# A graph network with a spectral convolution on Trainium2: an earlier third tap step, taps three tiles ahead, one copy moved to ScalarE, and tap spectra stored by pairs of frequencies

## The chip, the cores and the metric

The kernel runs on one core of one Trainium2 chip. The metric is device time in microseconds (us) of one execution of the whole program, everything in float32. A core has five engines with a queue of instructions each: TensorE (PE, matrix products; PEld is its loading of weights), VectorE (DVE), ScalarE (ACT), GpSimd (POOL) and SyncE (SP). SP and ScalarE also issue DMA transfers between DRAM and the on-chip memory (SBUF); the rows "SPq" and "ACTq" of a profile are such issues, and the transfers themselves run beside the engines. TensorE writes into PSUM, which has eight banks of 128 x 512 numbers. Engines run in order, each by its own queue, and wait for each other by semaphores.

## What is computed

x has 128 graphs of 128 nodes with 256 features, adj is 128 x 128 x 128. Cut to what matters here:

```python
# layer 0
h    = maximum(layernorm(x), 0)
c    = relu(bn1(conv1d(h, conv1_w)))            # 1 tap: a product over features
c    = bn2(conv1d(c, conv2_w, pad=8))           # 17 taps along the nodes, 256 -> 256
xc   = relu(c + h)
s    = h @ w_se.T + b_se;  A = exp(-dist(s)) * adj
xn   = A @ relu(h @ w_msg.T + b_msg)            # "x_nmp"
gi   = concat(xc, xn) @ w_ih.T + b_ih;  gh = h @ w_hh.T + b_hh
r, z = sigmoid(gi_r + gh_r), sigmoid(gi_z + gh_z)
x    = x + (1 - z) * tanh(gi_n + r * gh_n) + z * h
# layer 1: graph convolutions on five groups of the first 25 nodes
h    = maximum(layernorm(x), 0)
x    = x + sum_g softmax(fusion_w)[g] * graph_conv(graph_conv(h[:, g], W1[g]), W2[g])
```

## The kernel before

The graphs are handled in 32 blocks of four (`BB`). Layer 0 has three stages.

**Front.** The 17-tap convolution is done in the frequency domain, with windows of 80 points (`LW`) and so 40 pairs of real coefficients (`NP_`). For the first 64 graphs (16 blocks) each block goes through these helpers: `head_load` (x from DRAM, tile `ln`, five blocks ahead), `head_stats` (mean and variance on VectorE, L191 to L194, and a power by GpSimd, L196, tile `rs`), `head_norm` (VectorE, L202, four instructions), `head_turn` (eight transposes on TensorE, L212, and a ReLU by ScalarE, L213, into `ht`, which is also stored, L214), `head_conv1` (L226, with weights `wc1`) and `head_spectra` (L241, transform into the large tile `X`; L247 and L249 copy it from PSUM by VectorE and ScalarE).

Between these, the spectra of the taps are made, which fill TensorE while the blocks wait for other engines. There are eight tap tiles (c, q): 128 of the input channels and 64 of the output channels. `taps_load` brings a tile of taps (`w2`, 1 MB, two buffers), `weight_spectra` turns it in four steps of 16 products (L165, 32 records in the profile; only 17 of the array's 128 rows are used). Of each step's four banks three are evicted by ScalarE (L173) and one by VectorE (L171), and in the last step all four by ScalarE. After the last step ScalarE issues the store of the tile's spectra `sp` (2.5 MB) to the DRAM tensor `vd` (L175), and behind it the load of the next-but-one tile's taps (L155). `some_spectra` does one such step. `constants()` folds the batch norm into `wc1` and other constants; its first part runs on VectorE and GpSimd (L126 to L134, two powers of GpSimd, L128), its second needs TensorE (L138), ScalarE (L139) and VectorE (L140, L141). `constant_loads` issues three small loads on SP, `vec` (all biases and norms) among them.

In this stage all orders are written out by hand: the instructions stand in each engine's queue in the order of the calls.

**Spectral.** For each of 40 frequencies TensorE multiplies `X` with the tap spectra (L302, L312, L317: three complex-product terms). The spectra of two frequencies at a time come back from `vd` (L294, tile `v`, two loads of 512 KB, three buffers); GpSimd forms the sum `vs` (L309). The results go to DRAM (`yd`). Then the 64 other graphs pass through the heads and the spectral stage again. The heads of the second half begin within the first spectral stage.

**Gates.** A planner orders the rest. For each block: `messages` (L516; VectorE adds biases and forms `lr`, L517 to L529), `conv_out` (L498, L501, back from the frequency domain), `edge_terms` (L536, transposes of `lr`), `edges` (L548, and L553 on VectorE), `x_nmp` (L563; the result `xn` has two halves c, copied from PSUM by ScalarE for c = 0, L568, and by VectorE for c = 1, L566), `gate_inputs` (L586 to L589, tile `t`) and `gates` (L612, seven products of a Strassen scheme for each gate). `degrees` (L698 to L722) works out layer 1's degrees on VectorE beside the first block: long reductions of tensors that SP has just begun to load (`dga`, `dgb`, `dgc`).

Of the kernel before, what the change touches and what calls it, by code (L numbers as in the profile page):

```python
# [8 lines left out]
F32 = mybir.dt.float32  # L9
# [4 lines left out]
P = 128  # L14
# [6 lines left out]
LW = 80  # L21
# [53 lines left out]
def gnn_kernel(ctx: ExitStack, tc: tile.TileContext, io, out0: bass.AP, out1: bass.AP):  # L75
# [19 lines left out]
    def row(name, n):  # L95

        return bass.AP(tensor=io[name].tensor, offset=io[name].offset, ap=[[0, P], [1, n]])
# [14 lines left out]
    brz = cst.tile([P, 4], F32)  # L112

    def constant_loads():
        nc.sync.dma_start(vec, io["vec"])
        nc.sync.dma_start(wc1, io["wc1"].rearrange("(c p) o -> p c o", p=P))
        nc.sync.dma_start(fd, io["fd"])

# [27 lines left out]


    htd = [dram.tile([P, C, T], F32, tag=f"ht{i}", name=f"htd{i}") for i in range(NBLK)]
    vd = dram.tile([C, D // WCH, P, LW, WCH], F32, tag="vd", name="vd")
    yd = [dram.tile([HG, 2, LW, D], F32, tag=f"yd{h}", name=f"yd{h}") for h in range(NH)]  # L150

    def taps_load(pool, c, q, queue, split=1):
        w2 = pool.tile([P, WCH // 4, P], F32, tag="w2", name="w2", bufs=2)
        for t in range(0, WCH // 4, WCH // 4 // split):
            queue.dma_start(w2[:, t:t + WCH // 4 // split], io["w2t"][:, c, q, t:t + WCH // 4 // split])  # L155
        return w2

    def weight_spectra(pool, c, q, w2):

        sp = pool.tile([P, LW, WCH], F32, tag="sp", name="sp", bufs=2)  # L160
        for t in range(WCH // 16):
            ps = [bank() for _ in range(4)]
            for j in range(4):
                for r in range(4):
                    nc.tensor.matmul(ps[r][:, j * LW:(j + 1) * LW], w2[32 * r:32 * r + KW, 4 * t + j, :],  # L165
                                     gt[32 * r:32 * r + KW, :], start=True, stop=True)
            for r in range(4):
                o0 = t * 16 + 4 * r
                dst, s = sp[:, :, o0:o0 + 4], ps[r][:, :4 * LW].rearrange("p (j d) -> p d j", j=4)
                if r == 3 and t < WCH // 16 - 1:  # L170
                    nc.vector.tensor_copy(dst, s)  # L171
                else:
                    nc.scalar.copy(dst, s)  # L173
            yield
        nc.scalar.dma_start(vd[c, q], sp)  # L175


    xs, stats, hcs, h1s = {}, {}, {}, {}
# [5 lines left out]
    def head_stats(wk, i, behind=None):  # L184

        mv = wk.tile([P, BB, 2], F32, tag="mv", name="mv", bufs=3)
        st = wk.tile([P, BB, 6], F32, tag="st", name="st", bufs=2)
        if behind is not None:
            nc.scalar.copy(st[:, :, 0], behind[:, :, 0])
        for b in range(BB):  # L190
            nc.vector.bn_stats(st[:, b, :], xs[i][:, b, :])  # L191
            nc.vector.bn_aggr(mv[:, b, :], st[:, b, :])
        ve = wk.tile([P, BB], F32, tag="ve", name="ve", bufs=2)
        nc.vector.tensor_scalar(ve, mv[:, :, 1], EPS, None, op0=ALU.add)  # L194
        rs = wk.tile([P, BB], F32, tag="rs", name="rs", bufs=3)
        nc.gpsimd.tensor_tensor(rs, ve, mhalf, op=ALU.pow)  # L196
        stats[i] = mv, rs
# [87 lines left out]
    def spectral(bp, X, h, amid):  # L285

        for p0 in range(0, NP_, 4):
            amid.get(p0, lambda: None)()
            ys = bp.tile([P, 4, 2, D], F32, tag="ys", name="ys", bufs=2)
            for p in range(p0, p0 + 4):  # L290
                if p % 2 == 0:
                    v = bp.tile([P, C, D // WCH, 4, WCH], F32, tag="v", name="v", bufs=3)
                    for c in range(C):
                        nc.sync.dma_start(v[:, c], vd[c, :, :, 2 * p:2 * p + 4, :].rearrange("q i d o -> i q d o"))  # L294
                vr, vi = v[:, :, :, 2 * (p % 2), :], v[:, :, :, 2 * (p % 2) + 1, :]
                a, d = X[:, :, p, 0, :], X[:, :, p, 1, :]
                y = ys[:, p - p0]
                ps = bank()
                if p == 0:
                    for k, (u, w) in enumerate(((a, vr), (d, vi))):  # L300
                        for c in range(C):
                            nc.tensor.matmul(ps[:, k * D:(k + 1) * D], u[:, c], w[:, c], start=c == 0, stop=c == C - 1)  # L302
                    nc.scalar.copy(y.rearrange("p k o -> p (k o)"), ps)
                    continue

                s = bp.tile([P, C, P], F32, tag="s", name="s", bufs=2)
                nc.vector.scalar_tensor_tensor(s, a, -2.0, d, op0=ALU.mult, op1=ALU.subtract)  # L307
                vs = bp.tile([P, C, D // WCH, WCH], F32, tag="vs", name="vs", bufs=3)
                nc.gpsimd.tensor_tensor(vs, vr, vi, op=ALU.add)  # L309
                p1 = bank()  # L310
                for c in range(C):
                    nc.tensor.matmul(p1[:, :D], a[:, c], vs[:, c], start=c == 0, stop=c == C - 1)  # L312
                k1 = bp.tile([P, D], F32, tag="k1", name="k1", bufs=2)
                nc.scalar.copy(k1, p1[:, :D])
                for k, (u, w) in enumerate(((s, vi), (d, vr))):
                    for c in range(C):
                        nc.tensor.matmul(ps[:, k * D:(k + 1) * D], u[:, c], w[:, c], start=c == 0, stop=c == C - 1)  # L317
                nc.vector.tensor_tensor(y, ps.rearrange("p (k o) -> p k o", k=2),
                                        k1[:, None, :].to_broadcast([P, 2, D]), op=ALU.add)
            for w in range(2):  # L320
                nc.scalar.dma_start(yd[h][:, w, 2 * p0:2 * p0 + 8, :].rearrange("g d o -> g (d o)"),
                                    ys[w * HG:(w + 1) * HG].rearrange("p a k o -> p (a k o)"))
# [20 lines left out]
    with front as es:  # L343
# [7 lines left out]
        with ExitStack() as ws:  # L351

            ws.enter_context(tc.manual_schedule())

            xk = ws.enter_context(tc.tile_pool(name="xk", bufs=1, side="right"))
            wp = ws.enter_context(tc.tile_pool(name="wp", bufs=1))
            ahead = 5
            todo = [(c, q) for c in range(C) for q in range(D // WCH)]
            nc.scalar.dma_start(gt, io["gt"])
            taps = [taps_load(wp, *todo[0], nc.sync, split=4)]  # L360
            head_load(xk, ahead, 0, nc.scalar)
            spectra = []

            def some_spectra(k=1):
                for _ in range(k):
                    if not spectra and todo:
                        spectra.append(weight_spectra(wp, *todo.pop(0), taps.pop(0)))
                    if spectra and next(spectra[0], STOP) is STOP:
                        spectra.pop(0)
                        if len(todo) > 1:  # L370
                            taps.append(taps_load(wp, *todo[1], nc.scalar))
                        some_spectra()

            constant_loads()
            head_load(xk, ahead, 1, nc.sync)
            taps.append(taps_load(wp, *todo[1], nc.sync))
            for k in range(2, ahead):
                head_load(xk, ahead, k, nc.sync)
            nc.sync.dma_start(fw, row("fw", 5))
            head_stats(hk, 0)  # L380
            some_spectra()
            head_norm(0)
            some_spectra()
            head_turn(hk, 0)
            consts = constants()
            next(consts)
            some_spectra()
            head_stats(hk, 1)
            some_spectra()
            next(consts)  # L390
            head_norm(1)
            head_stats(hk, 2)
            some_spectra()
            heads(hk, xk, ahead, X, 0, some_spectra)
            while spectra or todo:
                some_spectra()
# [159 lines left out]
    def x_nmp(i):  # L556

        e, msg = A_s.pop(i), msgs.pop(i)
        xn = wk.tile([P, C, T], F32, tag="xn", name="xn", bufs=2)
        for c in range(C):  # L560
            ps = bank()
            for b in range(BB):
                nc.tensor.matmul(ps[:, b * N:(b + 1) * N], msg[:, b, c * P:(c + 1) * P], e[:, b, :],  # L563
                                 start=True, stop=True)
            if c:
                nc.vector.tensor_copy(xn[:, c, :], ps)  # L566
            else:
                nc.scalar.copy(xn[:, c, :], ps)  # L568
            yield
        xns[i] = xn  # L570
# [597 lines left out]
```

## Time and profile before

| | us |
|---|---|
| median of 3 runs (1916.35 to 1928.1) | 1919.29 |
| the profiled execution | 1919.48 |
| its span | 1917.7 |

The busy time of TensorE by stage, from the view of windows (us, of the span's start):

| stage | window | TensorE busy | VectorE busy | ScalarE busy | DMA share |
|---|---|---|---|---|---|
| front, first half | 0 to 173.3 | 160.55 of 173.30 | 113.24 | 88.02 | 0.81 |
| spectral, first half | 173.3 to 279.5 | 105.23 of 106.20 | 55.34 | 16.01 | 0.84 |
| heads, second half | 279.5 to 383 | 101.73 of 103.50 | 78.02 | 47.42 | 0.54 |
| spectral, second half | 383 to 489.5 | 105.72 of 106.50 | 50.54 | 16.52 | 0.81 |
| first block of the gates | 489.5 to 550 | 56.88 of 60.50 | 46.76 | 22.15 | 0.72 |
| the rest | 550 to 1917.7 | 1360.23 of 1367.70 | 960.04 | 530.39 | 0.33 to 0.37 |

How to read it: TensorE is busy nearly all the time, so time is lost where it is idle, and where its matmuls are slow: the same matmul takes twice as long in some places. A row of a timeline gives start, duration, engine, line, operation, output and inputs, how many, and in brackets the idle time before it and what ended it. "issue" means that the profile shows nothing that was waited for.

### The profile page before, as it was taken

To read this page: it belongs to the slowest core of one execution; us is meant where nothing else is said; L and a number is where in the kernel's file an instruction comes from. 1 tells how busy PE (TensorE), PEld (TensorE's weight loads), DVE (VectorE), ACT (ScalarE), POOL (GpSimd) and SP (SyncE) were. 2 spreads that over 40 slices of the span, in tenths; PEclk is the share of its full clock that TensorE was granted. 3 is DMA by queue.
4 is the path that set the end of the run, shared out by engine and by line. 5 is a ranking of instruction groups with operands and counts; after the bars stand their busy time and mean duration, and the time that the engine had idled before them with its cause. 6 is when DMAs were issued, how large, how long until landed. Compare 5 with 4: busy or idle time off the path is not lost.

```text
span 1917.7 us, 30432 instructions
## 1 busy us (share of the span) xinstructions
PE 1890.3 (99%) x10610; PEld 1646.4 (86%) x10610; DVE 1303.9 (68%) x3247; ACT 720.5 (38%) x1555; POOL 609.1 (32%) x678
## 2 busy tenths in 40 slices
PE   8999999999999999999999999999999999999998
PEld 7888889988788888888888888888888888888887
DVE  5676557744677777777666677777756677787643
ACT  4553114411333343343343443333343434334334
POOL 1012531255234334433322233433322233443300
PEclk9999999999999999999999999999999999999999
DMA  8786896379842333333234433233334434222135
GB/s 322 288 312 226 297 311 235 121 241 306 256 117 73 74 95 76 81 90 106 71 94 97 130 97 87 73 82 108 75 90 97 144 72 107 65 78 71 36 92 151
DMA packets 248872, 265.81 MB, mean 139 GB/s; under 512 B 106866, under 2 KB 223943, under 8 KB 244239
## 3 DMA queue, kind: packets, MB, share of 16 engines
q1 hardware_dynamic: 236639, 196.70, 36.9%
q10 hardware_dynamic: 12080, 67.16, 9.0%
q8 instruction: 85, 1.39, 0.3%
q14 instruction: 68, 0.56, 0.1%
HBM read 178.66 MB, written 85.14 MB: 138 GB/s over the span
## 4 chain that ended last, share of the span: by engine, by line
PE 88%; DMA 4%; DVE 4%; issue 2%; ACT 1%; POOL 1%; SPq 0%; ACTq 0%; POOLq 0%; DVEq 0%
PE bank L612 45%; PE bank L317 6%; PE bank L516 5%; PE bank L937 5%; PE bank L877 5%; PE bank L226 4%; PE bank L312 3%; PE bank L563 3%; PE bank L498 3%; PE bank L241 3%; PE bank L165 2%; PE bank L501 1%; PE bank L788 1%; PE bank L856 1%; DMA v<-vd 1%
## 5 line engine op out<-in xcount | busy, mean ns | idle before, releaser
L612 PE MATMUL bank<-t,sw 128*128 128x256 f32 x1152 | 291.6, 380 | 0.7 <-DVE u L504 0.7
L625 POOL TENSOR_TENSOR u<-u,m 128x256 f32<-128x256 f32 x128 | 93.2, 728 | 612.7 <-ACT m L623 545.0
L612 PEld LDWEIGHTS bank<-t,sw 128*128 128x128 f32 x1152 | 215.8, 191 | 31.1 <-issue 2.3
L612 PE MATMUL bank<-t,wih 128*128 128x256 f32 x768 | 197.2, 379 | 0.0
L612 PEld LDWEIGHTS bank<-t,wih 128*128 128x128 f32 x768 | 143.4, 190 | 19.3 <-issue 0.5
L309 POOL TENSOR_TENSOR vs<-v 128x512 f32<-128x512 f32 x78 | 101.3, 1318 | 114.8 <-DMA v<-vd 49.4
L516 PE MATMUL bank<-wms,ht 128*128 128x259 f32 x512 | 124.1, 385 | 0.0
L226 PE MATMUL bank<-wc,ht 128*128 128x256 f32 x512 | 121.4, 391 | 1.6 <-ACT ht L213 1.6
L612 PE MATMUL bank<-xn,wih 128*128 128x256 f32 x384 | 114.9, 381 | 3.6 <-DVE xn L566 3.6
L612 PE MATMUL bank<-t,whh 128*128 128x256 f32 x384 | 115.0, 381 | 0.0
L612 PE MATMUL bank<-xc,wih 128*128 128x256 f32 x384 | 114.8, 381 | 0.0
L937 PE MATMUL bank<-w,hh 128*125 128x256 f32 (+9 forms) x480 | 113.5, 380 | 1.0 <-DVE hh L882 1.0
L226 PEld LDWEIGHTS bank<-wc,ht 128*128 128x128 f32 x512 | 98.0, 196 | 16.7 <-ACT ht L213 3.5
L516 PEld LDWEIGHTS bank<-wms,ht 128*128 128x128 f32 x512 | 98.3, 192 | 15.1
L612 PE MATMUL bank<-ht,whh 128*128 128x256 f32 x384 | 109.9, 380 | 0.0
L877 PE MATMUL bank<-ax,w 128*128 128x500 f32 (+8 forms) x416 | 107.0, 396 | 0.7 <-DMA w<-in_w_dram 0.7
L520 ACT ACTIVATE msg<-msg 128x512 f32<-128x512 f32 x64 | 40.3, 630 | 174.1 <-DVE msg L517 174.1
L630 DVE TENSOR_TENSOR u<-bank,u 128x256 f32<-128x256 f32 x128 | 53.7, 420 | 73.6 <-PE bank L612 73.5
L196 POOL TENSOR_TENSOR rs<-ve,mhalf 128x4 f32<-128x4 f32 x32 | 32.3, 1009 | 217.8 <-DVE ve L194 217.8
L307 DVE SCALAR_TENSOR_TENSOR s<-X 128x256 f32<-128x256 f32 x78 | 47.3, 612 | 79.4 <-PE bank L317 79.1
L937 PEld LDWEIGHTS bank<-w,hh 128*125 128x125 f32 (+9 forms) x480 | 84.3, 177 | 19.2 <-DVE hh L882 1.4
L657 ACT ACTIVATE nn<-nn,vec 128x512 f32<-128x512 f32 x64 | 46.2, 722 | 133.4 <-DVE nn L656 133.4
(187 smaller groups left out, 4279.5 us busy)
## 6 DMA issues: line engine op xcount, KB each, us to landing
v<-vd SPq DMA_DIRECT2D x80, 512.0 KB
vd<-sp ACTq DMA_DIRECT2D x8, 2560.0 KB
yd<-ys ACTq DMA_DIRECT2D x40, 512.0 KB
w<-in_w_dram SPq DMA_DIRECT2D x40, 512.0 KB
htd<-ht ACTq DMA_DIRECT2D x32, 512.0 KB
ht<-htd SPq DMA_DIRECT2D x32, 512.0 KB
ym<-yd SPq DMA_DIRECT2D x32, 512.0 KB
xt<-in_xT_dram SPq DMA_DIRECT2D x32, 512.0 KB
```

The costliest lines, as they stand in the source:

```text
L226: nc.tensor.matmul(pv[:, bb, :], ht[:, c, b * N:(b + 1) * N], wc1[:, c, :], start=c == 0, stop=c == C - 1)
L241: nc.tensor.matmul(ps[:, bb * 2 * LW:(bb + 1) * 2 * LW], h1[:, 2 * h + bb, c * P:(c + 1) * P], fd, start=True, stop=True)
L309: nc.gpsimd.tensor_tensor(vs, vr, vi, op=ALU.add)
L312: nc.tensor.matmul(p1[:, :D], a[:, c], vs[:, c], start=c == 0, stop=c == C - 1)
L317: nc.tensor.matmul(ps[:, k * D:(k + 1) * D], u[:, c], w[:, c], start=c == 0, stop=c == C - 1)
L498: nc.tensor.matmul(ps[:, b * N:(b + 1) * N], ym[:, b, o * P:(o + 1) * P], idm, start=b == 0, stop=False)
L516: nc.tensor.matmul(ps[:, :D + 3], ht[:, c, b * N:(b + 1) * N], wms[:, c, :], start=c == 0, stop=c == C - 1)
L563: nc.tensor.matmul(ps[:, b * N:(b + 1) * N], msg[:, b, c * P:(c + 1) * P], e[:, b, :], start=True, stop=True)
L612: nc.tensor.matmul(ps, w, d, start=n == 0, stop=n == len(pairs) - 1)
L625: nc.gpsimd.tensor_tensor(got["u4"], got["u2"], got["m5"], op=ALU.add)
L877: nc.tensor.matmul(pv[:, q - q0, :], w1s[k5 + g][:, c, q * P:(q + 1) * P], xv[:, c], start=c == 0, stop=c == C - 1)
L937: nc.tensor.matmul(ps[:n1, :D], hh[:, q, at:at + n1], w2s[k5 + g][:, q, :], start=q == 0, stop=q == HID // P - 1)
```

## The change

Four edits, all but one in the front stage:

- The load of `vec` goes from SP to ScalarE's queue, behind `gt`. The first part of `constants()` comes ahead of the first tap step and of `head_norm(0)`; a third tap step comes ahead of the first transposes, and the step that stood after `constants()` goes.
- The tap tiles have three buffers and are loaded three ahead: one more load on SP in the beginning, and then each tile's end issues the load of the tile after the next two.
- `vd` is laid out by pairs of frequencies: a load of `v` reads 4 KB in a row for each of 128 partitions (before: four pieces of 1 KB); the store of a tile writes 20 pieces of 1 KB for each partition (before: one of 20 KB).
- For block 0, ScalarE copies both halves of `xn`.

```diff
@@ constant_loads @@
-        nc.sync.dma_start(vec, io["vec"])
@@ vd, taps_load @@
-    vd = dram.tile([C, D // WCH, P, LW, WCH], F32, tag="vd", name="vd")
+    vd = dram.tile([C, NP_ // 2, P, D // WCH, 4, WCH], F32, tag="vd", name="vd")
...
-        w2 = pool.tile([P, WCH // 4, P], F32, tag="w2", name="w2", bufs=2)
+        w2 = pool.tile([P, WCH // 4, P], F32, tag="w2", name="w2", bufs=3)
@@ weight_spectra @@
-        nc.scalar.dma_start(vd[c, q], sp)
+        nc.scalar.dma_start(vd[c, :, :, q].rearrange("u i d o -> i u (d o)"), sp.rearrange("p (u d) o -> p u (d o)", d=4))
@@ spectral @@
-                        nc.sync.dma_start(v[:, c], vd[c, :, :, 2 * p:2 * p + 4, :].rearrange("q i d o -> i q d o"))
+                        nc.sync.dma_start(v[:, c], vd[c, p // 2])
@@ front @@
             nc.scalar.dma_start(gt, io["gt"])
+            nc.scalar.dma_start(vec, io["vec"])
...
-                        if len(todo) > 1:
-                            taps.append(taps_load(wp, *todo[1], nc.scalar))
+                        if len(todo) > 2:
+                            taps.append(taps_load(wp, *todo[2], nc.scalar))
...
             nc.sync.dma_start(fw, row("fw", 5))
+            taps.append(taps_load(wp, *todo[2], nc.sync))
             head_stats(hk, 0)
+            consts = constants()
+            next(consts)
             some_spectra()
             head_norm(0)
             some_spectra()
+            some_spectra()
             head_turn(hk, 0)
-            consts = constants()
-            next(consts)
-            some_spectra()
             head_stats(hk, 1)
@@ x_nmp @@
-            if c:
+            if c and i:
                 nc.vector.tensor_copy(xn[:, c, :], ps)
```

In the built program TensorE's order differs only there (48 products of tap steps ahead of the first transposes, and 16 behind them). On VectorE L202 of block 0 now follows L126 to L134 and the first L171; around the first block of the gates the planner also moved the sums of `dgc` and `dgb`: the one of `dgb` stands ahead of the messages, three of `dgc` behind `lr`, and two scalings of `ae` ahead of L553.

## The prediction, before the changed kernel was run

> **What bounds the kernel.** I read the shares of busy time first, then TensorE's waits, then the timeline around each long wait. The profiled execution took 1919.48 us (span 1917.7 and 1.8 around it); the median of the three runs is 1919.29, so the two bases agree to 0.2 us, and every sum below starts from 1919.5.
>
> ```profile
> span 1917.7 us, 30432 instructions
> ...
> PE 1890.3 (99%) x10610; PEld 1646.4 (86%) x10610; DVE 1303.9 (68%) x3247; ACT 720.5 (38%) x1555; POOL 609.1 (32%) x678
> ```
>
> TensorE is idle for only 1917.7 - 1890.3 = 27.4 us. The change removes no matmul, so what it can win is part of these 27 us, and what a pause costs afterwards (below). TensorE's waits over the whole span, longest first (total us, times, longest):
>
> ```profile
> PE bank L165 <- DMA gt<-in_gt_dram: 3.9, 1, 3.9
> PE bank L612 <- DVE xn L566: 3.6, 1, 3.6
> PE bank L212 <- issue: 2.6, 1, 2.6
> PE bank L165 <- DMA w<-in_w2t_dram: 2.4, 1, 2.4
> PE bank L241 <- ACT X L249: 2.3, 1, 2.3
> ```
>
> The change aims at the second (xn), third (first transposes), fourth (taps) and perhaps fifth (tap spectra). The timeline of TensorE around the fourth (start, us, what, idle before it) shows that a pause costs more than itself:
>
> ```profile
> 66.42 1.09 PE L212 MATMUL bank<-ident,ln 128*128 128x128 f32 x8
> 69.94 1.13 PE L165 MATMUL bank<-gt,w 17*128 17x80 f32 x32 [2.42 <-DMA w<-in_w2t_dram]
> 71.00 4.11 PE L241 MATMUL bank<-fd,h 128*128 128x160 f32 x16
> ```
>
> The same 16 L241 matmuls took 2.44 us at 58.27: the pause of 2.42 us cost another 1.67 us of slow matmuls.
>
> **The Trainium skill.** (1) "TensorE: Matmul & The Clock Gate", Part 1, "What's actually happening": TensorE runs at half clock by default and after an idle window of about 3.4 us, at full clock after about 3.4 us of activity. The trace agrees on the factor (eight transposes: 2.25 us at 10.25, 1.09 at 66.42), but here already 2.4 us of pause brings the slow clock. (2) "DMA: Bandwidth & Descriptors", "Why small descriptors are slow (HBM only)": each packet carries a fixed overhead of about 3 cycles. The trace agrees in direction: the view of DMA traffic shows 126 packets of 20 KB (the tap spectra's store) and then 721 of mostly 1 KB (x loads) as
>
> ```profile
> DMA packets 126, 2.58 MB, mean 430 GB/s; under 512 B 0, under 2 KB 0, under 8 KB 0
> DMA packets 721, 0.74 MB, mean 368 GB/s; under 512 B 16, under 2 KB 718, under 8 KB 720
> ```
>
> (3) Same page, "Issuing engines are not separate DMA queues": all queues share 16 DMA engines. The trace agrees: from 149 to 151 us only ScalarE's queue moved data, though SP had issued three v loads from 148.57 on.
>
> **Part 1: three tap steps first, constants earlier, vec on ScalarE's queue.** Before, TensorE does two steps (3.90 to 7.62), waits for the normalised first block and turns it at 10.25. A third step is 32 records at the slow 58 ns, 1.86 us, which fits the hole of 2.6. But the order on VectorE changes too: constants() now stands before head_norm(0). VectorE before:
>
> ```profile
> 9.73 1.38 DVE L202 TENSOR_SCALAR ln<-ln,mv,rs 128x256 f32<-128x256 f32 x4 [0.83 <-POOL rs L196]
> ...
> 11.43 0.15 DVE L126 TENSOR_SCALAR bnve<-vec 128x2 f32<-128x2 f32 x1
> ...
> 14.31 0.42 DVE L134 COPY bnb<-bn 128x512 f32<-128x512 f32 x1
> ```
>
> From L126 to the end of L134 are 3.3 us, with two round trips to GpSimd (0.7 us each), and one 0.48 us copy L171. In the new order the chain starts after L194 (8.5 us), its first pow queues behind rs (8.66 to 9.69) and starts at 9.7; so bnb ends near 12.8, L171 near 13.3, and L202 starts near 13.2 instead of 9.73: +3.5 us. vec must have landed by 8.5; issued 1.2 us in, behind gt (landed 3.90, 3.2 us after its issue), it should. ln0 is issued 0.43 later on ScalarE's queue, but waits for the first taps' data anyway: up to +0.3. The transposes then start near 13.7; what follows them is one step shorter (1.86). conv1 (L226) of block 0 starts 3.5 - 1.86 = **1.6 us later**. Bounds 0 and +3. TensorE is busy for 9.75, 9.90 and 9.23 of the ten microseconds each from 10 to 40, so it stays lost. SP issues one load fewer before wc1 and one more (1 MB of taps, 0.33 to 0.43 us) behind fw at 10.5; SP's next loads wait for L212 anyway (103.8 us of such waits), so this costs nothing while x is five blocks ahead.
>
> **Part 2: taps three tiles ahead.** At 56.21 ScalarE issues 1 MB of taps just behind the 2.5 MB store of 55.84; it lands near 69.9, 13.7 us later, and TensorE waits. One tile earlier (a tile is some 17 us) the load is hidden by a whole tile of work: **-2.42 - 1.67 = -4.1 us**; bounds -4.1 and -1. Next late would be a bank, 0.2 to 0.4 us.
>
> **Part 3: spectra by two frequencies.** A v load goes from 512 pieces of 1 KB to 128 of 4 KB, the store from 128 of 20 KB to 2560 of 1 KB. Taking 430 GB/s for the large pieces and 357 (the v loads' own 0.54 MB in 1.5 us from 152) for 1 KB, a v load falls from 1.47 to 1.22 us, 80 of them by 20 us of DMA time; but TensorE idles only 106.20 - 105.23 and 106.50 - 105.72 in the two spectral stages, 1.8 us in all, some of it for VectorE. I take **-0.6** (0 to -1.8). The store goes from 6.1 to 7.1 us at 368 GB/s. That counts once: the chain of waits has
>
> ```profile
> 139.26 9.29 DMA vd<-sp
> 148.57 6.21 DMA v<-vd
> ```
>
> and then L249 at 155.25, for which TensorE waits 2.33 us: +1.0 for the store and -0.5 for the two loads, **+0.5** (-1 to +4, if 1 KB writes to DRAM are slower than the 1 KB reads measured).
>
> **Part 4: xn by ScalarE.** ScalarE is idle from 501.0 to 503.05, so the copy is free there. VectorE before:
>
> ```profile
> 507.02 1.53 DVE L698 TENSOR_REDUCE dinv<-dga 128x53 f32<-128x1325 f32 x1 [5.18 <-DMA dga<-in_adjF_dram]
> 508.47 0.68 DVE L566 COPY xn<-bank 128x512 f32<-128x512 f32 x1
> ```
>
> The copy stood behind a reduction that waits for a load. TensorE lost 3.58 us there and then 2.9 us to the slow clock: the 16 records from 509.21 to 515.53 took 6.3 us instead of 16 x 0.216 = 3.5. But this is not all won: L586 to L589 (t from xn), the messages' evictions L517 and lr still stand behind L698, and L536 needs lr. From 508.47 until lr is done (L529, 518.65) VectorE works 10.2 us with one wait of 1.19, and from 515 to 530 it is over 99% busy. Its chain shortens by the copy (0.61 us from start to start), by the 1.2 us of waiting for dgc (the longer dgb sum now fills it) and, for lr alone, by three of the sums (0.6) that move behind it; the edge product L553 has two scalings more before it (0.5). So lr comes some 2.4 us earlier and L553 some 1.3, and TensorE, which reaches L536 earlier still, waits there and cools again: **-1.5** (0 to -6.4).
>
> **Sum.** +1.6 - 4.1 - 0.6 + 0.5 - 1.5 = -4.1: 1915.4, **1915 us**. This case's own range is 1910 to 1919.
>
> **Rivals.** *Slower: the store fills ScalarE's queue.* SP's run of v loads at 148.57 took 0.4 to 0.5 us an issue for three, then 1.22 and 2.70: roughly 100 pieces per DMA engine are taken in, then the issuer is held. The new store is 2560/16 = 160; some 60 x 16 must move first, 0.98 MB, 2.7 us at 368 GB/s, plus 0.7 until data flows: 3.4 us in which ScalarE evicts nothing. One such hold is in the trace:
>
> ```profile
> 36.53 0.45 ACTq L175 DMA_DIRECT2D vd<-sp  x1
> 37.02 2.00 ACTq L155 DMA_DIRECT2D w<-in_w2t_dram  x1
> 39.12 1.08 ACT L173 COPY sp<-bank 128x320 f32<-128x320 f32 x3 [2.98 <-issue]
> ```
>
> It cost TensorE 1.25 us idle and 1.5 us slow (L226 in 5.13 instead of 3.62), 2.75. Seven more stores at that price are 19 us, half of them absorbed 10: -4 + 10 = +6, 1925, up to 1934. It decides from two held stores on (2 x 2.75 exceeds 4.1). Against it: at 55.84 and 103.99 the pair of issues took 0.8 us, and a store's issue so far costs 0.33 whatever its 2.5 MB. *All bubbles close:* part 1 at 0, parts 2 to 4 near their good ends (-4.1, -1.8, -1, -3) and the hold at 37 us gone (-2.75): -12.6, 1907. For it: ScalarE's evictions; against it: the order on VectorE. *Nothing moves:* part 2 saved, part 1 and the later store take it back: 1918 to 1920.
>
> **Chances.** Main case 0.50, held stores 0.25, all bubbles 0.13, nothing 0.12. 1% (19 us) is about what a measurement of this kernel tells from no change. Below 1900 needs 19 of the 27 idle us with their slow matmuls, 0.10; above 1938.5 needs every store held or slow writes beside, 0.12. Leaving out a tenth on each side gives 1905 to 1930.
>
> **What would show it.** Right: no wait L165 on in_w2t; L202 near 13.2 us and L212 still waiting 3 to 4 us; L536 waiting for lr; v loads of 4 KB near 430 GB/s. Wrong: ScalarE's issue rows of taps or htd at 2 us or more behind each store, with TensorE's waits on L173 or L249; a wait on xn gone without another in its place; slow matmuls in new places.

## The result, and the profile after

| | us |
|---|---|
| kernel before, median of 6 runs | 1918.63 |
| changed kernel, median of 6 runs (1934.82 to 1940.13) | 1937.24 |
| ratio after / before, with its 95% interval | 1.009 (1.0067 to 1.0113) |
| profiled execution after, its span | 1939.18, 1937.4 |

The changed kernel is 18.6 us (0.9%) slower, where 1915 was predicted and 1905 to 1930 given as the range. The page of the changed kernel begins

```profile
span 1937.4 us, 30432 instructions
...
PE 1897.4 (98%) x10610; PEld 1652.5 (85%) x10610; DVE 1308.0 (68%) x3246; ACT 720.8 (37%) x1556; POOL 610.6 (32%) x678
```

The span grew by 19.7 us: TensorE is idle for 40.0 us instead of 27.4, and busy for 7.1 us more with the same 10,610 matmuls, which therefore ran slower. TensorE's waits, longest first (us in total, times, longest one), name new things. The waits for xn and for the taps are gone; line numbers in the front stage are one lower than before.

```profile
PE bank L164 <- ACT sp L172: 9.5, 4, 3.8
PE bank L211 <- DMA ln<-in_x_dram: 6.2, 1, 6.2
PE bank L225 <- ACT ht L212: 4.8, 6, 1.9
PE bank L164 <- DMA gt<-in_gt_dram: 4.0, 1, 4.0
PE bank L537 <- DVE lr L530: 2.5, 1, 2.5
```

Four waits of 9.5 us in all are for ScalarE's copies of the tap spectra out of PSUM. ScalarE's timeline around the second store shows why (start, us, what, idle before it):

```profile
41.44 0.33 ACTq L213 DMA_DIRECT2D htd<-ht  x1
41.81 0.45 ACTq L174 DMA_DIRECT2D vd<-sp  x1
42.35 5.35 ACTq L154 DMA_DIRECT2D w<-in_w2t_dram  x1
47.75 1.08 ACT L172 COPY sp<-bank 128x320 f32<-128x320 f32 x3 [6.33 <-issue]
```

The store's own issue takes 0.45 us. The *next* issue, the taps, takes 5.35, and the copy behind it starts only then. TensorE needs that copy's bank:

```profile
44.05 0.41 PE L164 MATMUL bank<-gt,w 17*128 17x80 f32 x2 [0.36 <-DVE X L246]
48.23 1.99 PE L164 MATMUL bank<-gt,w 17*128 17x80 f32 x26 [3.76 <-ACT sp L172]
50.15 5.36 PE L225 MATMUL bank<-wc,ht 128*128 128x256 f32 x16
```

It idles for 3.76 us, and its matmuls are slow for 7 us after that: the 16 L225 take 5.36 us instead of 3.62, and the mean granted clock is 0.67 from 45 to 50 us and 0.65 from 50 to 55, where it is 1.00 from 40 to 45. The other taps issues behind a store take 3.92, 3.30, 4.86 and 3.42 us.

The start of conv1 (L226 before, L225 after), block by block, says where the 19.7 us arose:

| point | later than before, us | what lies ahead of it |
|---|---|---|
| block 0 | 4.25 | first transposes late |
| block 1, then 2 | 5.28, then 9.29 | held issue of 5.35 |
| block 3, then 4 | 9.51, then 14.04 | held issue of 3.30 |
| block 5 | 9.93 | the old pause for the taps is gone: -4.1 |
| block 6, then 7 | 13.92, then 19.87 | held issues of 4.86 and 3.42 |
| blocks 8 to 12 | 19.6 to 19.9 | stores with no taps load behind them |
| first spectral matmul | 22.0 | last store, and an htd issue of 3.40 behind it |
| first matmul of the gates | 20.4 | two spectral stages |
| end | 19.7 | gates |

The other large item is the start. VectorE's timeline after:

```profile
8.73 0.43 DVE L190 BATCH_NORM_STATS2 st<-ln 128x6 f32<-128x256 f32 x1 [8.73 <-DMA ln<-in_x_dram]
...
15.70 1.37 DVE L201 TENSOR_SCALAR ln<-ln,mv,rs 128x256 f32<-128x256 f32 x4
```

The first x block landed at 8.73 us; before it was 6.08. The stage that loads the spectra did as intended. The chain of waits around the last store gives the durations of the store and of the first v load:

```profile
158.88 10.14 DMA vd<-sp
169.04 4.82 DMA v<-vd
```

### The profile page after: what moved, and what is told of

It is laid out like the page before. It is cut to its first block, busy times and chain, and to the rows that moved or that the text cites. A ratio compares the mean times of both kernels' runs of the same rounds, so it can differ in the third digit from the quotient of the medians.

```text
span 1937.4 us, 30432 instructions
## 1 busy us (share of the span) xinstructions
PE 1897.4 (98%) x10610; PEld 1652.5 (85%) x10610; DVE 1308.0 (68%) x3246; ACT 720.8 (37%) x1556; POOL 610.6 (32%) x678
## 4 chain that ended last, share of the span: by engine, by line
PE 88%; DVE 4%; DMA 3%; issue 2%; ACTq 1%; ACT 1%; POOL 0%; SPq 0%; POOLq 0%; DVEq 0%
PE bank L613 44%; PE bank L316 7%; PE bank L517 5%; PE bank L938 5%; PE bank L878 4%; PE bank L225 4%; PE bank L311 3%; PE bank L564 3%; PE bank L499 3%; PE bank L240 2%; PE bank L164 1%; PE bank L502 1%; PE bank L789 1%; PE bank L857 1%; PE bank L211 1%
## 5 line engine op out<-in xcount | busy, mean ns | idle before, releaser
L613 PEld LDWEIGHTS bank<-t,wih 128*128 128x128 f32 x768 | 144.0, 191 | 19.6 <-issue 0.5
L225 PE MATMUL bank<-wc,ht 128*128 128x256 f32 x512 | 123.7, 396 | 4.8 <-ACT ht L212 4.8
L225 PEld LDWEIGHTS bank<-wc,ht 128*128 128x128 f32 x512 | 99.0, 198 | 21.3 <-ACT ht L212 7.6
L306 DVE SCALAR_TENSOR_TENSOR s<-X 128x256 f32<-128x256 f32 x78 | 55.6, 716 | 75.2 <-PE bank L316 75.0
L938 PEld LDWEIGHTS bank<-w,hh 128*125 128x125 f32 (+9 forms) x480 | 84.3, 178 | 19.6 <-DVE hh L883 1.9
```

What stands on the lines that cost most here:

```text
L225: nc.tensor.matmul(pv[:, bb, :], ht[:, c, b * N:(b + 1) * N], wc1[:, c, :], start=c == 0, stop=c == C - 1)
L613: nc.tensor.matmul(ps, w, d, start=n == 0, stop=n == len(pairs) - 1)
L938: nc.tensor.matmul(ps[:n1, :D], hh[:, q, at:at + n1], w2s[k5 + g][:, q, :], start=q == 0, stop=q == HID // P - 1)
```

## The experiments

Each kernel was timed in turn with the kernel before; the ratio is against it, since its median moved between 1918.1 and 1919.6 from batch to batch.

| run | median us | ratio to before | interval |
|---|---|---|---|
| a1_old_layout | 1915.34 | 0.998 | 0.9968 to 0.9992 |
| a2_layout_alone | 1934.56 | 1.0082 | 1.0053 to 1.0111 |
| c1_taps_first | 1930.7 | 1.0063 | 1.0042 to 1.0085 |
| a4_store_on_sp | 1910.74 | 0.9958 | 0.9945 to 0.997 |
| e1_old_layout_sp | 1909.28 | 0.9955 | 0.9941 to 0.9969 |
| d3_pieces_2k | 1926.15 | 1.0038 | 1.0023 to 1.0052 |
| d1_sp_vec_back | 1908.67 | 0.9949 | 0.9932 to 0.9966 |
| d2_sp_late_consts | 1903.72 | 0.9924 | 0.9906 to 0.9942 |
| e2_sp_two_steps | 1905.4 | 0.993 | 0.9916 to 0.9945 |
| t_taps_alone | 1913.85 | 0.9976 | 0.9968 to 0.9985 |
| x_xn_alone | 1918.95 | 0.9996 | 0.998 to 1.0012 |

The theory at the outset: the store of 2560 pieces holds the next issue of its queue, and on ScalarE that blocks the eviction of PSUM. The rival: writing 1-KB pieces takes the bandwidth that the loads need.

### Is it the layout? Taken out, and put in alone

The changed kernel with the old `vd`:

```diff
-    vd = dram.tile([C, NP_ // 2, P, D // WCH, 4, WCH], F32, tag="vd", name="vd")
+    vd = dram.tile([C, D // WCH, P, LW, WCH], F32, tag="vd", name="vd")
...
-        nc.scalar.dma_start(vd[c, :, :, q].rearrange("u i d o -> i u (d o)"), sp.rearrange("p (u d) o -> p u (d o)", d=4))
+        nc.scalar.dma_start(vd[c, q], sp)
...
-                        nc.sync.dma_start(v[:, c], vd[c, p // 2])
+                        nc.sync.dma_start(v[:, c], vd[c, :, :, 2 * p:2 * p + 4, :].rearrange("q i d o -> i q d o"))
```

> The changed kernel with the tap spectra in the old layout (store 128 pieces of 20 KB, loads of 1 KB pieces); start, taps and xn as changed. Held issues (theory): ScalarE's issue of the taps behind each store falls from 3.3 to 5.4 us to at most 2, the four pauses of TensorE before L164 (9.5 us, with their slow matmuls about 15 to 18) go, and the time is 1919 to 1923. Start (rival: constants and vec cost most of it): 1933 to 1936. Bandwidth (rival: the small pieces load the DMA engines): also 1919 to 1923, so this run tells the layout from the rest, not held issues from bandwidth.

Measured 1915.34. In its trace the taps issues behind the stores take 0.39 to 1.70 us, and no wait of L164 for L172 is left. The kernel before with the three opposite lines and nothing else:

> The kernel before with the new layout of the tap spectra alone. Held issues: five to six taps issues of 3 to 5 us behind the stores, TensorE waits on L173, and the taps still come late once; 1932 to 1940. Start (rival): 1917 to 1919. Bandwidth (rival): 1925 to 1940, with TensorE waiting for data (taps, ln) and not for ScalarE's copies.

Measured 1934.56. Its taps issues behind the stores take 3.33 to 5.52 us, and TensorE's longest wait is

```profile
PE bank L165 <- ACT sp L173: 10.1, 4, 3.9
```

The late taps that were also expected are not there: no wait for the taps is left in this run. Between them the two runs settle the place: the layout alone costs 0.8% (15.9 us; taken out of the changed kernel it is worth 21.9), all the rest together gains 0.2%. The first came out 4 us below its expectation. At conv1 of block 0 it is 4.7 us behind the kernel before; by block 3 it has won back 2.3 (the issue that took 2.00 us in the kernel before takes 0.60), at block 5 the taps' 4.1 more, and at the first spectral matmul it is ahead (171.48, against 173.14).

### Bandwidth or held issue? The store on another queue, and another order

```diff
-        nc.scalar.dma_start(vd[c, :, :, q].rearrange(...
+        nc.sync.dma_start(vd[c, :, :, q].rearrange(...
```

> The changed kernel with the eight stores of spectra issued by SP and no longer by ScalarE; pieces, layout and bytes as in the change. Held issues: SP is held now and computes nothing, ScalarE's taps issues are back at 0.4 to 1 us, the pauses before L164 go: 1918 to 1924. Bandwidth (rival): the same pieces run on the same 16 DMA engines, so nothing is won: 1934 to 1938. Start (rival): 1934 to 1938.

Measured 1910.74: the same bytes in the same pieces, and 26.5 us less. That is 7 us below the range expected; at the first spectral matmul this run is 28.8 us ahead of the changed kernel, so the held issues had cost more than was thought. The traffic while a store is under way is alike in both, first the changed kernel (45 to 47 us), then this one (42 to 44):

```profile
DMA packets 751, 0.77 MB, mean 386 GB/s; under 512 B 1, under 2 KB 750, under 8 KB 751
```

```profile
DMA packets 756, 0.77 MB, mean 387 GB/s; under 512 B 0, under 2 KB 756, under 8 KB 756
```

So the rival falls. The hold is not gone but has moved to SP, whose next issue, an x load, is now the long one, while ScalarE's taps issue takes 1.23 us. SP's timeline, then ScalarE's:

```profile
39.26 0.37 SPq L174 DMA_DIRECT2D vd<-sp  x1
39.73 7.11 SPq L181 DMA_DIRECT2D ln<-in_x_dram  x1
```

```profile
40.68 1.23 ACTq L154 DMA_DIRECT2D w<-in_w2t_dram  x1
```

SP computes nothing and is several x blocks ahead, so nobody waits for these 7 us.

The other order keeps both issues on ScalarE, the taps load ahead of the store:

```diff
             yield
+        if len(todo) > 2:
+            taps.append(taps_load(pool, *todo[2], nc.scalar))
         nc.scalar.dma_start(vd[c, :, :, q].rearrange(...
```

> The changed kernel with the load of the next taps issued ahead of the store of the spectra, both by ScalarE as before; nothing else. If what is held is the issue that follows the store (theory), the issue that follows is now one of htd some 6 to 17 us later, which finds the queue free: no issue over 1.5 us but the last (htd behind the eighth store, about 3.4 us), 1918 to 1924. If the store's own issue is what holds ScalarE, or bandwidth, it stays at 1933 to 1938.

Measured 1930.7, which misses both ranges, and the trace shows what the expectation overlooked. ScalarE's timeline around the third store:

```profile
58.41 0.34 ACTq L154 DMA_DIRECT2D w<-in_w2t_dram  x1
58.84 0.39 ACTq L176 DMA_DIRECT2D vd<-sp  x1
...
61.57 5.97 ACTq L215 DMA_DIRECT2D htd<-ht  x1
67.58 1.08 ACT L172 COPY sp<-bank 128x320 f32<-128x320 f32 x3 [6.05 <-issue]
```

The taps issue is short, and htd, 2.7 us behind the store, is held in its place. Behind the second store htd came 9.9 us later, at 51.99, and took 0.78. So it is whichever issue comes next on that queue while the store is being moved.

### Is it the number of pieces? 1280 of 2 KB

```diff
-    vd = dram.tile([C, NP_ // 2, P, D // WCH, 4, WCH], ...)
+    vd = dram.tile([C, NP_ // 4, P, D // WCH, 8, WCH], ...)
...
-                        nc.sync.dma_start(v[:, c], vd[c, p // 2])
+                        nc.sync.dma_start(v[:, c], vd[c, p // 4, :, :, 2 * (p % 4):2 * (p % 4) + 4])
```

(The store is cut with d=8 to match.)

> The changed kernel with the spectra in DRAM by four frequencies: ScalarE's store has 1280 pieces of 2 KB (80 per DMA engine) where it had 2560 of 1 KB (160), the same bytes; each v load is 512 pieces of 1 KB again. If a queue takes in about 100 pieces per DMA engine and holds the next issue until older ones are moved, most of the following taps issues (128 pieces, 8 more per engine) are not held: 1 us or less each, TensorE's waits on sp L172 in the front stage below 2 us together, and a time of 1912 to 1918. If it is scattered writing or pieces under some size that holds the issue, about half of each hold stays (2 us behind several stores) and the time is 1924 to 1930. If the hold went by bytes, nothing would change: 1934 to 1940.

The holds behaved as the count says: the five taps issues took 0.68, 1.63, 0.74, 1.00 and 0.77 us, 4.8 in all, where they took 20.9, and TensorE's waits on L172 fell from 9.5 to 0.9 us. The longest:

```profile
43.34 1.34 ACTq L174 DMA_DIRECT2D vd<-sp  x1
44.77 1.63 ACTq L154 DMA_DIRECT2D w<-in_w2t_dram  x1
```

The time, 1926.15, is nevertheless outside the 1912 to 1918 of this theory and inside the 1924 to 1930 of the other. The trace puts the rest elsewhere: its first x block landed at 10.79 us, and from the first spectral matmul to the gates it took 324.2 us, the changed kernel 314.8. There TensorE waited for GpSimd's sums of v (5.5 us in six waits), in the first spectral stage at

```profile
231.77 1.91 PE L311 MATMUL bank<-vs,X 128*128 128x256 f32 x4 [2.04 <-POOL vs L308]
```

The v loads, four pieces of 1 KB at steps of 2 KB, take 0.62 us each to issue (median) instead of 0.35. So the median alone would have named the wrong theory; the issue rows tell them apart. This profile is the slowest of nine executions, so how much of the 324.2 us belongs to the kernel is not known.

The pieces of this run are also twice as large, so a limit by size would do as well here. Against it speaks the run of v loads in the prediction: three loads of 1-KB pieces were taken in before the fourth was held. The changed kernel's own trace narrows the count. While its third taps issue was held (65.77 to 69.07), ScalarE's queue (q10) moved

```profile
q10 hardware_dynamic: 1014, 1.04, 88.8%
```

that is 1014 of the store's 2560 pieces. When the issue got through, 1546 were left, 97 per engine; for the fifth it was 94, close to the "roughly 100" of the prediction's rival. It is not one fixed number: on SP, the hold of 7.11 us ended with 47 per engine left.

### What the layout is worth where no one is held

The changed kernel with the old layout *and* the store on SP, `nc.sync.dma_start(vd[c, q], sp)`:

> The changed kernel with the spectra in DRAM as before (128 pieces of 20 KB for a store, 512 of 1 KB for a v load) and the store on SP's queue; against the run with the new layout and the store on SP (1910.7) it prices the layout alone, with no issue held on ScalarE. Theory: the 4-KB loads are worth 0.6 to 1.8 us in the spectral stages as predicted, and a few held issues that the old store too put on ScalarE go: 1911.5 to 1913. Rival: nearly all of what the store on SP brought against the old layout on ScalarE (1915.3 to 1910.7) is the layout's: 1914.5 to 1916. Second rival: the layout is worth nothing once the store is off ScalarE: 1910 to 1911.

Measured 1909.28, against 1910.74 with the new layout; the ratios, 0.9955 and 0.9958, can't be told apart. The time lies below all three ranges, nearest the second rival: the layout brings nothing to the median that these runs can tell. Taking the store off ScalarE does, with the old layout too: 0.998 to 0.9955. The run with the old layout on ScalarE has a wait of 2.9 us for ScalarE's copy L248 behind the last store, which is absent with either store on SP. In the profiled executions the spectral part is shorter with 4-KB loads (314.1 to 315.8 us in seven kernels, 316.3 to 323.1 in the five with the old layout), but those are one execution each, and the one of e1 was the slowest of its ten.

### The start

With the store on SP, `vec` is loaded by SP again:

```diff
     def constant_loads():
+        nc.sync.dma_start(vec, io["vec"])
...
-            nc.scalar.dma_start(vec, io["vec"])
```

> The changed kernel with the store on SP's queue and the 128-piece load of vec back at the head of SP's constants. Theory: the vec issue ahead of it delayed the first x load by 0.45 us, enough to fall behind SP's wc1, so that it lands at 6.1 us again where it landed at 8.2 to 8.7; the first normalisation L201 then starts near 13.2 us and the first transposes near 13.8, conv1 of block 0 at 21 to 21.7 us (it was 23.7 with the store on SP), and the time is 2 to 2.7 us below the kernel with the store on SP alone: 1908 to 1909. Rival: the x load is late because of the taps ahead of it, whatever vec does: it lands at 8 us again and the time stays at 1910.7. vec itself may then land later than 8.5 us and hold the constants on VectorE, up to 2 us of the gain lost.

Measured 1908.67, as expected; but its ratio, 0.9949 beside 0.9958, can't be told from that of the store on SP alone. What shows the effect is the landing of x. VectorE's and TensorE's timelines of this kernel:

```profile
6.22 0.43 DVE L191 BATCH_NORM_STATS2 st<-ln 128x6 f32<-128x256 f32 x1 [6.22 <-DMA ln<-in_x_dram]
...
13.19 1.37 DVE L202 TENSOR_SCALAR ln<-ln,mv,rs 128x256 f32<-128x256 f32 x4
```

```profile
13.85 2.10 PE L212 MATMUL bank<-ident,ln 128*128 128x128 f32 x8 [3.62 <-DVE ln L202]
...
21.77 6.38 PE L226 MATMUL bank<-wc,ht 128*128 128x256 f32 x16
```

Over all profiles, the first x block landed at 6.08, 6.16, 6.22, 6.23, 6.47, 7.11 and 7.40 us with `vec` on SP, and at 7.13, 8.16, 8.73, 9.16, 9.42 and 10.79 with `vec` ahead of it on ScalarE: means of 6.5 and 8.9. With an issue of 0.45 us ahead of it, it landed 2.4 us later in the mean; in the pair that differs in this alone, 8.16 instead of 6.22.

Next, the first stage of `constants()` goes behind the first transposes again, with three tap steps ahead of them:

```diff
-            consts = constants()
-            next(consts)
             some_spectra()
             head_norm(0)
             some_spectra()
             some_spectra()
             head_turn(hk, 0)
+            consts = constants()
+            next(consts)
```

> As the run with the store and vec on SP, and the first stage of constants() again behind the first transposes, with the third tap step still ahead of them. Theory: without the constants' two round trips to GpSimd ahead of it the first L201 starts at 9.7 to 10.3 us as in the kernel before, the transposes follow the third tap step at 10.3 to 11 us, and conv1 of block 0 starts at 18.2 to 19 us, 2 to 3 us before that of the kernel with vec alone put back: 1905 to 1907. Rival: what follows the transposes then waits for bnb (L137) as the step that covered its chain is gone: the idle time moves from L211 to L137, conv1 starts at 20 us or later, and the time is 1908 to 1910.

Measured 1903.72, below the range expected, 0.76% below the kernel before and the fastest of all. In this profile x landed late (7.40), and the third step could not run in the hole, since its bank was freed by VectorE's copy, which stood behind the statistics of x:

```profile
10.27 2.01 PE L165 MATMUL bank<-gt,w 17*128 17x80 f32 x32 [2.63 <-DVE sp L171]
```

The rival's place was right in part: TensorE waits 0.47 us for bnb. To price the third step, the same kernel with two:

> The best version so far (store and vec on SP, constants behind the first transposes) with two tap steps ahead of the first transposes instead of three, which is the order of the kernel before: it prices the third step. Theory: the hole of 2.6 us ahead of the transposes stays empty and the step runs later, conv1 of block 0 starts 1.3 to 1.9 us later relative to the landing of the first x block, and the time is 1905 to 1906 against 1903.7. Rival: the third step only moves TensorE's wait to the bank that VectorE frees, and is worth nothing: 1903 to 1904.5.

Measured 1905.4, inside the theory's range, but with a ratio of 0.993 beside 0.9924: no difference that these runs can tell. What counts at the start is to keep the constants off VectorE's way to the first transposes (1908.67 to 1903.72). This last kernel has the start of the kernel before, so it also prices the changed start as a whole, with the store on SP in both: 1910.74 against 1905.4, 5.3 us.

### The other two parts alone

The kernel before with taps three ahead (bufs=3, one load behind fw, `todo[2]`):

> The kernel before with the taps loaded three tiles ahead (third buffer, one load more behind fw) and nothing else. Theory (the step as predicted): the pause of 2.42 us for the taps and the 1.67 us of slow matmuls behind it go, and nothing else is late: 4.1 us below the kernel before, 1914 to 1915.5. Rival: the loads that are moved ahead take bandwidth from x in the front stage and another pause comes instead: 1917 to 1919.

Measured 1913.85, 4.3 us below 1918.14 and a little better than expected. The wait on in_w2t is absent, and conv1 of the fifth block starts at 59.86 and of the sixth at 68.99, 9.1 us apart where it was 13.2.

The kernel before with `if c and i:` for the copy of xn:

> The kernel before with the first block's xn copied by ScalarE and nothing else. Theory (the step as predicted): TensorE no longer waits 3.6 us for xn, reaches lr earlier and waits there, and the edge product comes about 1.5 us sooner: 1917 to 1918.2. Rival: the wait for xn takes the place of nothing and the slow matmuls behind it go too: 1912 to 1914. Third: VectorE's chain to e decides alone and the copy was no part of it: 1918.7, no change.

Measured 1918.95, a ratio of 0.9996 (0.998 to 1.0012): no difference, though one of 1.5 us would be too small to show. In its profile the wait for xn is gone and two others are there, for lr and for u:

```profile
521.91 0.41 PE L536 MATMUL bank<-ident,lr 128*128 128x128 f32 x2 [1.28 <-DVE lr L529]
```

```profile
563.26 0.70 PE L612 MATMUL bank<-t,sw 128*128 128x256 f32 x2 [2.16 <-DVE u L504]
```

Counted from the first matmul of the gates, the second block's product with e comes 4.5 us earlier than before, and the sixth block's only 2.3. The run with the taps alone, which leaves xn as it was, is 3.2 us ahead at the sixth block: its wait for xn was 1.3 us, not 3.58, and in the run with the layout alone it was 2.8. So this wait differs between profiles that share the copy, and the copy's worth lies below what these runs resolve.

## Why the prediction was wrong

**The bound and the reading of pauses** held: TensorE's idle time, and slow matmuls behind each pause, decide.

**Part 1, predicted +1.6 (0 to 3), was +4.25** at conv1 of block 0, and 5.3 in the medians with the store on SP. The order on VectorE was read rightly. With `vec` back on SP, L202 starts at 13.19 (predicted 13.2), the transposes at 13.85 (13.7), conv1 at 21.77 (20.02 + 1.6 = 21.6). The term that failed is x's landing, "up to +0.3": it was +2.65 in this profile. The bound was argued from x waiting for the first taps' data anyway; what its place in the queue costs was not worked out.

**Part 2, predicted -4.1, was -4.1**: alone it gained 4.3. In the changed kernel the shift also falls by 4.1 between the fifth and sixth conv1 (14.04 to 9.93), but that can't be credited to it: with the layout alone, and taps two tiles ahead, it falls as much (12.46 to 8.35), presumably because the held issues delay TensorE until the taps are there.

**Part 3, predicted +0.5 - 0.6, was near +20 in the profile (+15.9 alone, 21.9 when taken out), and is the step that failed.** Its working priced the store by its bytes: 6.1 to 7.1 us of transfer, counted once at the end. That size was right (the last store 9.29 to 10.14, +0.85 for +1.0; the v load 6.21 to 4.82; from the first spectral matmul to the gates -1.6, within 0 to -1.8), though v loads ran at 397 GB/s (172 to 174 us), not 430. Left out of the sum was what the store does to the issue behind it: that was put at nothing. The rival had it, with the right mechanism and place, a hold of 3.4 us (measured 3.3 to 5.4) and 2.75 us of TensorE for each, and its sign, an issue of taps or htd of 2 us or more, came behind six of the eight stores. Three things went wrong in weighing it. The sentence "a store's issue so far costs 0.33 whatever its 2.5 MB" took evidence from stores of 128 pieces, 8 per DMA engine, for one of 160. It also looked at the store's own issue, which stayed at 0.38 to 1.0, when the held one is the next. And "half of them absorbed" was a guess: from block 1 to block 7 four held issues moved conv1 by 18.7 us with the taps' gain set aside (19.87 - 5.28 + 4.1), 4.7 each, since slow matmuls follow each pause. The rival's own figures, 19 us unabsorbed, less 4, and 2.65 more at the start, would have been 1937. That this comes so near is in part luck: it has seven stores at 2.75 us, where four cost 4.7, the first some 1.0 and the last some 2.4; and the 2.75 itself takes 1.25 us of idle time from a place where the trace has 0.77.

The Trainium skill has two statements on this. "DMA: Bandwidth & Descriptors", "Anatomy of one DMA — SWDGE (gpsimd) path", calls descriptor generation small and variable and says that many can be emitted before the cost shows (of GpSimd's DMAs; these were ScalarE's and SP's); "Issuing engines are not separate DMA queues" says that several issuing engines save only the sequencer's time to initiate a DMA, usually small beside the DMA itself. Here a held issue on ScalarE was up to 5.97 us of an engine that other engines wait for, and moving the store was worth 26.5 us. The measurement decides.

**Part 4, predicted -1.5 (0 to -6.4), was -0.7 in the profile** (20.4 to 19.7 from the gates' first matmul to the end) and within noise alone, so its size is neither confirmed nor refuted. That TensorE would wait for lr instead was right: 2.5 us.

**Shown and not shown.** Shown: the layout causes the loss (out and in), through held issues on ScalarE (moved with the queue, moved with the order), and halving the number of pieces while doubling their size removes most of the hold. Not shown: the exact limit, which lies above the 80 pieces per engine of the smaller store and below the 160 of the larger, and whether it is counted per engine; behind the old store, too, one issue took 2.00 us. Why a 0.45 us later issue lands x 2.4 us later is also open: in the profile, SP's wc loads are issued and move data in that time, but their order was not changed in a run. The prediction's remark that 1% is about what a measurement can tell was too cautious: the interval of the 0.9% is 0.23% to either side.

## What to carry to other kernels

Count a DMA's pieces per engine as well as its bytes, and put a transfer of thousands of pieces on a queue whose engine evicts nothing: in these runs its price was paid by the next issue behind it. When a rival's mechanism has been seen once in the trace, price it from there at full, and do not weigh it down with evidence from a case that lacks its cause. A layout that makes loads larger pays only if those loads are what someone waits for.

## What the runs showed of the hardware

- An issue within 0.15 us behind a store of 2560 pieces took 3.3 to 5.5 us on ScalarE and 3.1 to 8.3 on SP; behind one of 1280 pieces 0.7 to 1.6, and behind one of 128 pieces 0.4 to 2.0. Eight us or more after a store of 2560 pieces it took 0.33 to 0.78.
- The store's own issue did not show it: 0.37 to 1.11 us with 2560 pieces.
- Writes of 1 KB ran at 386 GB/s, those of 20 KB at 430 in the kernel before: a tenth of the rate. The held issues cost far more.
- A pause of 2.64 us (at 69.64 in the changed kernel) was followed by L240 in 4.01 us instead of 2.44.
